# Four edits in a linear-attention and neighbourhood-attention kernel: column-ordered evacuation of the second group's queries, PSUM pairs in another order, shorter ring copies, and a later load of half the next image

## The chip, the cores and the metric

The program runs on one core of one Trainium2 chip. It is one launch that does the whole batch of sixteen images. The metric is device microseconds from start to end, the median of three runs. One more execution was taken with the hardware profiler; every duration below is from that one.

## The reference

Two residual layers act on x of shape (16, 64, 64, 256), and each starts with a group norm over 32 groups of channels.

```
x = x + linear_attention(gn(x))       # 8 heads of 32, softmax of q over d, of k over the 4096 pixels
x = x + neighbourhood(gn(x))          # 8 heads of 32, 7x7 window around each pixel
```

In the second layer, each pixel's query is multiplied with the 49 keys of its window, to which a learnt position embedding is added: for heads 0 to 3 it depends on the row of the window, for heads 4 to 7 on the column.

```
kp = unfold(k, 7) + e                        # e: emb0 by window row, emb1 by window column
attn = softmax(einsum(q, kp)) ;  out = einsum(unfold(v, 7), attn)
```

Everything is float32.

## The kernel before

The sixteen images are done one after the other in one loop. Channels lie on the partitions in two halves of 128, pixels in the free dimension, cut into eight strips of 512 (strip 0 is made of the image's two edges, 5 and 3 columns wide; the other strips are 8 columns by 64 rows). One image goes through these stages:

1. **Layer 0** (`layer0`): queries and keys by matmul (L514), `exp` on ACT (L518), the context matrix (L532), transposes (L546), and the output product (L587), which DVE adds to the image (L596) while it gathers statistics (L473).
2. **Positions and values** of layer 1: `positional_products` and `positional` put the products of queries and position embeddings into rows 0 to 63 of the tile `qq`; `store_rings` (L658) copies them to DRAM buffers `pos` so that `load_rings` (L665, L666) can read them back as a band with a different shift in each row; `values` (L677, L680) computes v and stores it to the DRAM buffer `vpad` (L685, L690), from which `load_window` (L731) fetches the windows `vw`.
3. **Keys and queries of head group 0** (`keys_queries(b, 0, x)`): eight groups of eight matmul passes (L703), four for keys and four for queries, each into two PSUM banks; ACT (L619) or DVE (L621) moves each result of 32 partitions by 512 to SBUF, adding the bias. Keys go to `kaug`, queries to `qq`.
4. **Attention of group 0** (`local_attention(b, 0, ...)`): four units of sixteen image columns, each with nine row blocks c. TensorE computes scores (L760) into a double PSUM tile, ACT takes `exp` (L768), TensorE sums weights and weighted values (L791) into the four single banks, which it first clears (L778, once a unit). At a unit's end `finish` divides and POOL adds to the output (L824).
5. **The same two stages for head group 1.** In its attention the statistics and the norm of the next image are worked in.

The order of instructions on each of PE, ACT, DVE and SP is the order in which the program issues them (`manual_schedule`), and each engine runs its own in order. All transfers are issued by SP, one queue in program order. Semaphores hold an instruction until the tiles that it needs are there or free.

[...] `double` is two tiles of two banks (pd), `single` four tiles of one (ps). `banks()` hands out four pairs in turn and says which engine evacuates each half (0 is DVE, 1 is ACT):

```
i = turn[1] % 4
if i % 2:
    return single[i - 1 : i + 1], (0, 1)
return [double[i // 2][:, j] for j in range(2)], (i // 2, i // 2)
```

So the turns are pd0 (both halves by DVE), ps0 and ps1 (one each), pd1 (both by ACT), ps2 and ps3 (one each). A double tile counts as one tile: its evacuation starts when the matmuls of both halves are done. `psum2()` hands out the double tiles alternately to the scores.

`qq` holds a group-0 query as (row, column) and a group-1 query as (column, row). A strip's result comes out of the matmul as 64 rows of 8 columns in both groups. `evacuate` therefore writes, for group 1, each element 64 elements (256 bytes) away from the one before it.

`between0` and `between1` are called by `local_attention` after each of the five steps g of each unit i; they issue loads, stores and statistics of the next image at that point of the order. Before the change the next image's second half is loaded by `load_half(b + 1, 1)` (L463, eight transfers of 256 KB) ahead of `keys_queries(b, 0, x)`.

Of the kernel before, what the change touches and what calls it, by code (L numbers as in the profile page):

```python
# [20 lines left out]
W = 64  # L21
C = 256
HEADS, HD = 8, 32
NS = 8
# [331 lines left out]
def attention_fast(tc, io, ok):  # L356
# [3 lines left out]
    with ExitStack() as ctx:  # L360
# [11 lines left out]
        def banks():  # L372

            i = turn[1] % 4
            turn[1] += 1
            if i % 2:
                return single[i - 1 : i + 1], (0, 1)
            return [double[i // 2][:, j] for j in range(2)], (i // 2, i // 2)

        def bank(name):  # L380
            return psum2()[:, 0]
# [114 lines left out]
        def by_rows(a, like):  # L496

            return a.rearrange("p (g r) w -> p g r w", g=4) if len(like.shape) == 4 else a
# [117 lines left out]
        def evacuate(i, dst, src, bias):  # L616

            if i:
                nc.scalar.activation(dst, src, AF.Identity, bias=bias)  # L619
            else:  # L620
                nc.vector.tensor_scalar(dst, src, bias, None, ALU.add)  # L621
# [27 lines left out]
        def store_rings():  # L649

            line = SLOTS * 4 * W
            for hg in range(2):
                for a in range(4):
                    for o in (0, RING):
                        row = pos[hg][RING * a, o]
                        dst = bass.AP(row.tensor, row.offset, [[W, 4 * KS], [line + 4 * W, RING], [1, W]])
                        src = qq[32 * hg : 32 * hg + 4 * KS, 0, 1024 * a : 1024 * (a + 1)]
                        nc.sync.dma_start(dst, src)  # L658

        def load_rings(hg):  # L660
# [33 lines left out]
        def keys_queries(b, hg, x):  # L694

            for what in range(2):
                for i in range(0, NS, 2):
                    ps, engines = banks()
                    pair = KEYED[i : i + 2]
                    wgt = wq if what else wk  # L700
                    for a in range(2):
                        for k in range(2):
                            nc.tensor.matmul(  # L703
                                ps[a],
                                wgt[:, k, hg * P : (hg + 1) * P],
                                x[k][:, strip(pair[a])],
                                start=(k == 0),
                                stop=(k == 1),
                            )
                    for a in range(2):  # L710
                        for h in range(4):
                            rows = slice(h * HD, (h + 1) * HD)
                            d0 = 64 * (h % 2)
                            for u, p0, m, w, view in pieces(pair[a]):
                                src = view(ps[a][rows])
                                if what:
                                    dst = placed(qq[d0 : d0 + HD, h // 2], hg)[:, :, w : w + m]
                                else:
                                    dst = kaug[h // 2][d0 : d0 + HD, u, PAD : PAD + W, p0 : p0 + m]
                                evacuate(engines[a], by_rows(dst, src), src, bias[rows, 2 * what + hg : 2 * what + hg + 1])  # L720

        def load_window(b, hg, t):

# [130 lines left out]
        with tc.manual_schedule(engines=ORDERED):  # L854
            x, xn = halves(0)
            st = stats_tile("st0_0")
            for k in range(2):
                load_half(0, k)
            for k in range(2):
                for s in ORDER:  # L860
                    strip_stats(st, x, k, s)
            gn = n.group_stats(st, 1e-5, small, bank, "0_0")
            xtok = {q: load_tokens(0, q) for q in range(2)}
            for s in ORDER[:2]:
                normalise(xn, x, *gn, s)
            for b in range(B):
                more = b + 1 < B
                x, xn = halves(b)
                st = layer0(b, x, xn, *gn, xtok, 2)
                mean, rstd = n.group_stats(st, 1e-5, small, bank, f"1_{b}")  # L870
                scale(wpos, n.wpos, rstd)
                pairs = [ORDER[i : i + 2] for i in range(0, NS, 2)]
                positional_products(0, x, pairs[0])
                pb = bank("fold")
                fold_bias(mean, wpos, (4,), pb)
                scale(wv, n.wv_sb, rstd)
                for i in range(4):
                    if i < 3:
                        positional_products(i + 1, x, pairs[i + 1])
                    positional(i, pairs[i])  # L880
                pv = bank("foldv")
                for k in range(2):
                    nc.tensor.matmul(
                        pv[:, :C], mean[:, k : k + 1].to_broadcast([P, P]), wv[:, k], start=(k == 0), stop=(k == 1)
                    )
                nc.vector.tensor_tensor(bv, n.bv_sb, pv[:, :C], ALU.subtract)
                store_rings()
                for i, s in enumerate(KEYED):
                    values(b, s, x)
                    if i == 1:  # L890
                        scale(wk, n.wk_sb, rstd)
                        scale(wq, n.wq_sb, rstd)
                    if i == 3:
                        load_rings(0)
                pb = bank("fold2")
                fold_bias(mean, wk, (0, 1), pb)
                fold_bias(mean, wq, (2, 3), pb)
                vw = {i: load_window(b, 0, UNITS[i]) for i in range(2)}
                if more:
                    load_half(b + 1, 1)  # L900
                    st = stats_tile(f"st0_{b + 1}")
                    x_next, xn_next = halves(b + 1)
                keys_queries(b, 0, x)
                y = [xn[0], x[1]]
                vw1 = {}

                def store_out(hg, i):

                    for s in ((3,), (4, 5), (6, 7), (1, 2, 0))[i]:
                        nc.sync.dma_start(out[b, :, hg, strip(s)], y[hg][:, strip(s)])  # L910

                def between0(i, g):
                    if g == 4:
                        if i >= 2:
                            vw1[i - 2] = load_window(b, 1, UNITS[i - 2])
                        store_out(0, i)
                    if more and i and g < 3 and 3 * (i - 1) + g < NS:
                        strip_stats(st, x_next, 1, ORDER[3 * (i - 1) + g])

                local_attention(b, 0, x, y, vw, lambda: load_rings(1), between0)  # L920
                keys_queries(b, 1, x)
                if more:
                    load_half(b + 1, 0)
                steps, gn, xtok = None, [], {}

                def between1(i, g):
                    nonlocal steps
                    if g == 4:
                        if more and i >= 2:
                            xtok[i - 2] = load_tokens(b + 1, i - 2)  # L930
                        store_out(1, i)
                    if not more:
                        return
                    if i == 1 and g < 4:
                        for s in ORDER[2 * g : 2 * g + 2]:
                            strip_stats(st, x_next, 0, s)
                    if i == 2 and g == 0:
                        steps = n.group_steps(st, 1e-5, small, next_bank, f"0_{b + 1}", gn)
                    if i == 2 and g < 3:
                        next(steps, None)  # L940
                    if i == 3 and g in (1, 2):
                        normalise(xn_next, x_next, *gn, ORDER[g - 1])

                local_attention(b, 1, x, y, vw1, lambda: None, between1)

            m = small.tile([P, 4], F32, tag="range", name="range")
            nc.gpsimd.memset(m, 0.0)
            for i, total in enumerate((tops, others)):
                nc.vector.tensor_reduce(m[:, i : i + 1], total, AX.X, ALU.add)
            nc.vector.tensor_reduce(m[:, 3:4], m[:, :3], AX.X, ALU.add)  # L950
            pm = bank("range_t")
            nc.tensor.transpose(pm[:1, :P], m[:, 3:4], n.ident)
            worst = small.tile([1, 1], F32, tag="worst", name="worst")
            nc.vector.tensor_reduce(worst, pm[:1, :P], AX.X, ALU.add)
            nc.vector.tensor_scalar(ok, worst, 1e30, None, ALU.is_le)
# [376 lines left out]
```

## Time and profile before

| what | value |
|---|---|
| median of three runs | 6140.36 us (6137.88 to 6141.98) |
| the profiled execution, its time and its span | 6124.67 us, 6122.9 us |
| PE busy | 5477.6 us (89% of the span) |
| PE weight loads busy | 3748.6 us (61%) |
| DVE, ACT, POOL busy | 2963.6 us (48%), 2358.4 us (39%), 1029.9 us (17%) |
| mean granted TensorE clock | 0.964 of full |
| moved by DMA | 536.12 MB, 88 GB/s mean |

Engines overlap, so the busy shares do not add up. One image takes about 378 us. A time such as "1517.20" is in us from the span's start. In a timeline row the first number is the start, the second the length, then engine, line, operation, tiles and shapes, and in brackets the idle time before the row with what ended it. In a row of waits the numbers are the total, how often, and the longest.

### The profile page before, as it was taken

The numbers are of one execution on the slowest core, as the hardware profiler recorded it, in microseconds if no ns is written. First come the engines' busy times: TensorE is split into PE (matmuls) and PEld (weight loads), VectorE is DVE, ScalarE is ACT, GpSimd is POOL, SyncE is SP. The second block draws the span as 40 slices with busy tenths as digits, with TensorE's granted clock in tenths as the row PEclk, the third lists the DMA queues.
The fourth block names the chain that finished last, engine by engine and source line by source line (L and its number), as shares of the span: only waits on it lengthen the run. The fifth ranks groups of instructions, "written<-read, shape, count | busy, mean of one in ns | idle before, by whom it ended". The sixth has DMA issues, their size and how long they took to land.

```text
span 6122.9 us, 171756 instructions
## 1 busy us (share of the span) xinstructions
PE 5477.6 (89%) x76913; PEld 3748.6 (61%) x76913; DVE 2963.6 (48%) x5034; ACT 2358.4 (39%) x3233; POOL 1029.9 (17%) x1945
## 2 busy tenths in 40 slices
PE   4989999898998989889898998988989999898997
PEld 2565665655656556665666656566565665656656
DVE  2544545545355454554544554454544545445354
ACT  0251443515335153351623425244252443515335
POOL 2012120211202112021120201212012120211202
PEclk9999999999999999999999999999999999999999
DMA  4341723416244252442515434163341723417234
GB/s 114 83 96 37 138 77 87 104 44 137 59 93 108 50 121 58 104 98 64 115 49 116 92 79 101 43 126 87 84 96 37 136 79 86 103 37 145 59 79 81
DMA packets 772876, 536.12 MB, mean 88 GB/s; under 512 B 276240, under 2 KB 703504, under 8 KB 769552
## 3 DMA queue, kind: packets, MB, share of 16 engines
q1 hardware_dynamic: 772128, 525.04, 38.8%
q8 instruction: 605, 9.91, 0.7%
q14 instruction: 143, 1.17, 0.1%
HBM read 357.02 MB, written 167.90 MB: 86 GB/s over the span
## 4 chain that ended last, share of the span: by engine, by line
PE 79%; ACT 6%; DMA 5%; SPq 4%; issue 4%; DVE 2%; POOL 0%; ACTq 0%; DVEq 0%; POOLq 0%
PE pd L760 15%; PE ps L791 15%; PE pd L514 14%; PE ps L532 7%; ACT qq L619 5%; PE pd L703 4%; PE pd L587 4%; PE ps L587 4%; PE ps L703 3%; PE pd L677 3%; PE ps L677 3%; PE ps L630 2%; DMA vpad<-v 2%; PE ps L546 2%; DMA vw<-vpad 2%
## 5 line engine op out<-in xcount | busy, mean ns | idle before, releaser
L768 ACT ACTIVATE e<-pd 128x896 f32<-128x896 f32 (+2 forms) x1152 | 926.5, 839 | 1078.3 <-PE pd L760 1077.3
L760 PE MATMUL pd<-qq,kaug 64*64 64x224 f32 (+5 forms) x27648 | 1044.8, 293 | 313.0 <-ACT qq L619 152.6
L760 PEld LDWEIGHTS pd<-qq,kaug 64*64 64x64 f32 x27648 | 918.9, 139 | 453.0 <-ACT qq L619 179.1
L514 PE MATMUL pd<-wqkv,img 128*128 128x512 f32 x2048 | 923.0, 595 | 1.6 <-DVE img L283 1.6
L791 PE MATMUL ps<-e,ones 128*32 128x112 f32 (+1 forms) x18432 | 835.6, 253 | 58.5 <-issue 57.9
L791 PE MATMUL ps<-e,vw 128*32 128x112 f32 (+1 forms) x18432 | 838.9, 256 | 54.0 <-issue 53.5
L804 DVE STREAM_TRANSPOSE r<-ps 128x512 f32<-128x512 f32 x256 | 168.7, 696 | 1415.1 <-PE ps L791 1415.1
L619 ACT ACTIVATE qq<-ps,bias 32x512 f32<-32x512 f32 (+2 forms) x544 | 370.1, 725 | 759.2 <-PE ps L630 711.6
L518 ACT ACTIVATE eq<-pd 128x1024 f32<-128x1024 f32 x256 | 261.9, 1023 | 943.5 <-PE pd L514 943.4
L451 POOL TENSOR_TENSOR others<-others,rc 128x16 f32<-128x16 f32 x256 | 113.0, 441 | 3045.1 <-DVE rc L809 3045.1
L514 PEld LDWEIGHTS pd<-wqkv,img 128*128 128x128 f32 x2048 | 372.6, 191 | 380.2 <-issue 352.8
L791 PEld LDWEIGHTS ps<-e,vw 128*32 128x32 f32 x18432 | 494.4, 111 | 139.9 <-issue 101.9
L791 PEld LDWEIGHTS ps<-e,ones 128*32 128x32 f32 x18432 | 536.8, 112 | 68.8 <-issue 67.9
L521 DVE TENSOR_REDUCE qz<-eq 128x16 f32<-128x512 f32 x256 | 175.5, 685 | 830.0 <-ACT eq L518 830.0
L532 PE MATMUL ps<-xtok,eq 128*128 128x257 f32 x2048 | 486.1, 380 | 0.0
L532 PEld LDWEIGHTS ps<-xtok,eq 128*128 128x128 f32 x2048 | 386.1, 190 | 149.0 <-issue 107.2
L824 POOL TENSOR_TENSOR img<-img,r 128x320 f32<-128x320 f32 (+1 forms) x512 | 421.5, 843 | 165.2 <-DVE rc L809 161.4
L619 ACT ACTIVATE kaug<-ps,bias 32x192 f32<-32x192 f32 (+2 forms) x384 | 196.8, 551 | 633.3 <-PE ps L703 630.0
L621 DVE TENSOR_SCALAR qq<-ps,bias 32x512 f32<-32x512 f32 x384 | 351.7, 916 | 8.7
L473 DVE BATCH_NORM_STATS2 st<-img 128x6 f32<-128x512 f32 x512 | 321.2, 677 | 66.4 <-DMA img<-in_xc 66.3
L524 POOL TENSOR_TENSOR eq<-eq,qr 128x512 f32<-128x512 f32 x256 | 274.7, 1073 | 30.7 <-DVE qr L523 1.2
L621 DVE TENSOR_SCALAR qq<-pd,bias 32x512 f32<-32x512 f32 x256 | 236.0, 922 | 29.7 <-PE pd L703 24.8
(126 smaller groups left out, 6269.8 us busy)
## 6 DMA issues: line engine op xcount, KB each, us to landing
vw<-vpad SPq DMA_DIRECT2D x512, 288.0 KB
img<-in_xc SPq DMA_DIRECT2D x256, 256.0 KB
xtok<-in_xt SPq DMA_DIRECT2D x64, 1024.0 KB
out<-img SPq DMA_DIRECT2D x256, 256.0 KB
vpad<-v SPq DMA_DIRECT2D x112, 512.0 KB
qq<-pos SPq DMA_DIRECT2D x128, 256.0 KB
qq<-in_ring SPq DMA_DIRECT2D x128, 256.0 KB
pos<-qq SPq DMA_DIRECT2D x256, 112.0 KB
```

Source lines behind the costliest of these rows:

```text
L473: nc.vector.bn_stats(st[:, k, s], x[k][:, strip(s)])
L514: nc.tensor.matmul(ps[:, t], xn[k][:, n0 : n0 + P], n.wqkv_sb[:, k, : 2 * C], start=(k == 0), stop=(k == 1))
L532: nc.tensor.matmul(pc[hg][:, : C + 1], eq[p][:, t, C + hg * P : C + (hg + 1) * P], xtok[p // 4][:, 2 * (p % 4) + t], start=(p == 0 and t = ...
L587: nc.tensor.matmul(py[co], w2[:, hg, co * P : (co + 1) * P], qq[:, hg, strip(s)], start=(hg == 0), stop=(hg == 1),)
L619: nc.scalar.activation(dst, src, AF.Identity, bias=bias)
L621: nc.vector.tensor_scalar(dst, src, bias, None, ALU.add)
L677: nc.tensor.matmul(pi[:, t], x[k][:, n0 : n0 + P], wv[:, k], start=(k == 0), stop=(k == 1))
L703: nc.tensor.matmul(ps[a], wgt[:, k, hg * P : (hg + 1) * P], x[k][:, strip(pair[a])], start=(k == 0), stop=(k == 1),)
L760: nc.tensor.matmul(to, kaug[pl][rows, u, 8 * c : 8 * c + 8].rearrange("p r w -> p (r w)"), q, start=True, stop=True,)
L768: nc.scalar.activation(e, ps[:, :, : 2 * m], AF.Exp)
L791: nc.tensor.matmul(dst, ones if to is zs[j] else vw[:, j, c, h * HD : (h + 1) * HD], pr, start=False, stop=(c == NB - 1),)
L824: nc.gpsimd.tensor_tensor(yv, xv, by_rows(add[:, :, a - w0 : e - w0], xv), ALU.add)
```

## The change

There are four edits.

- **Columns.** In `keys_queries`, for the queries of group 1 alone, both sides of the evacuation are reordered so that columns are the outer loop and rows the inner one. The destination in `qq` is then one contiguous run (512 elements, or 320 and 192 for the two pieces of strip 0), and the source in PSUM is read with a step of 8 elements (5 or 3 in strip 0).
- **Pairs.** `banks()` hands out pd0, pd1, ps0 with ps1, ps2 with ps3. It is used by L587, by `values` and by `keys_queries`. Which engine evacuates which tile stays the same.
- **Ring copies.** Each of the four pieces of a head group is still copied twice by `store_rings`, but the second copy holds its last 6 rows only, not 16 (42 KB, not 112 KB); the full copy now comes first.
- **Half image.** `load_half(b + 1, 1)` goes. Its eight strips are issued in `between0`, four in unit 0 and four in unit 1, after steps 0 to 3. The statistics of these strips, which stood in units 1 to 3 (three, three and two), now stand in units 2 and 3 (four each).

```
--- before.py
+++ after.py
@@ banks
             turn[1] += 1
-            if i % 2:
-                return single[i - 1 : i + 1], (0, 1)
-            return [double[i // 2][:, j] for j in range(2)], (i // 2, i // 2)
+            if i >= 2:
+                return single[2 * i - 4 : 2 * i - 2], (0, 1)
+            return [double[i][:, j] for j in range(2)], (i, i)
@@ store_rings
-                    for o in (0, RING):
-                        row = pos[hg][RING * a, o]
-                        dst = bass.AP(row.tensor, row.offset, [[W, 4 * KS], [line + 4 * W, RING], [1, W]])
-                        src = qq[32 * hg : 32 * hg + 4 * KS, 0, 1024 * a : 1024 * (a + 1)]
+                    for o, r in ((RING, 0), (0, RING - KS + 1)):
+                        row = pos[hg][RING * a + r, o + r]
+                        dst = bass.AP(row.tensor, row.offset, [[W, 4 * KS], [line + 4 * W, RING - r], [1, W]])
+                        src = qq[32 * hg : 32 * hg + 4 * KS, 0, W * (RING * a + r) : W * RING * (a + 1)]
                         nc.sync.dma_start(dst, src)
@@ keys_queries
-                                evacuate(engines[a], by_rows(dst, src), src, bias[rows, 2 * what + hg : 2 * what + hg + 1])
+                                dst = by_rows(dst, src)
+                                if what and hg:
+                                    order = "p r w -> p w r" if len(src.shape) == 3 else "p g r w -> p w g r"
+                                    dst, src = dst.rearrange(order), src.rearrange(order)
+                                evacuate(engines[a], dst, src, bias[rows, 2 * what + hg : 2 * what + hg + 1])
@@ attention_fast
                 if more:
-                    load_half(b + 1, 1)
                     st = stats_tile(f"st0_{b + 1}")
@@ between0
-                    if more and i and g < 3 and 3 * (i - 1) + g < NS:
-                        strip_stats(st, x_next, 1, ORDER[3 * (i - 1) + g])
+                    if more and g < 4:
+                        s = ORDER[4 * (i % 2) + g]
+                        if i < 2:
+                            nc.sync.dma_start(x_next[1][:, strip(s)], xc[b + 1, :, 1, strip(s)])
+                        else:
+                            strip_stats(st, x_next, 1, s)
```

## The prediction

> **What bounds the kernel now.** I read the busy shares first (PE 89%), then the waits of PE, then the timelines of one image around each wait, then instruction durations by shape. The PE waits that the change can touch:
>
> ```profile
> PE pd L760 <- ACT qq L619: 152.6, 32, 6.8
> PE ps L791 <- issue: 111.4, 73, 3.3
> PE pd L760 <- ACT e L768: 79.7, 32, 2.5
> PE pd L760 <- issue: 72.8, 49, 3.1
> ```
>
> The first and third come 32 times, twice an image: after each `keys_queries`, PE stands until ACT has emptied PSUM. The second and fourth are stalls inside the attention that no semaphore explains. PE at the two seams of image 3 (counted from 0), group 0 then group 1:
>
> ```profile
> 1414.74 3.60 PE L703 MATMUL ps<-img,wqn 128*128 128x512 f32 x8
> 1421.07 1.59 PE L760 MATMUL pd<-qq,kaug 64*64 64x80 f32 x48 [2.73 <-ACT qq L619]
> ...
> 1513.60 3.60 PE L703 MATMUL ps<-img,wqn 128*128 128x512 f32 x8
> 1523.99 2.79 PE L760 MATMUL pd<-qq,kaug 64*64 64x80 f32 x48 [6.79 <-ACT qq L619]
> 1529.27 3.27 PE L760 MATMUL pd<-qq,kaug 64*64 64x140 f32 x48 [2.50 <-ACT e L768]
> ```
>
> ACT at the second seam:
>
> ```profile
> 1510.37 4.55 ACT L619 ACTIVATE qq<-ps,bias 32x512 f32<-32x512 f32 x4 [1.28 <-PE ps L703]
> 1514.93 9.01 ACT L619 ACTIVATE qq<-pd,bias 32x512 f32<-32x512 f32 x8
> 1523.96 4.64 ACT L619 ACTIVATE qq<-ps,bias 32x320 f32<-32x320 f32 x8
> 1528.62 1.41 ACT L768 ACTIVATE e<-pd 128x512 f32<-128x512 f32 x2
> ```
>
> Call E the end of the last L703 (1517.20). ACT evacuates without a gap to E+11.4; PE's first scores wait for pd1 (E+6.8), the third for the first `exp` (E+12.1). ACT's sixteen query evacuations set the end here. DVE ends at E+7.5, so it doesn't. By shape in that stage:
>
> ```profile
> L619 ACT ACTIVATE qq<-pd,bias 32x512 f32<-32x512 f32 x8 | 8.9, 1115 | 0.1
> L619 ACT ACTIVATE kaug<-pd,bias 32x512 f32<-32x512 f32 x8 | 5.4, 678 | 0.8 <-PE pd L703 0.7
> ```
>
> Same size, same source: 678 ns into a contiguous row, 1115 ns with a 256-byte step in SBUF (741 ns in group 0, runs of 8).
>
> The chain of waits also shows "DMA vpad<-v", "DMA vw<-vpad" and "DMA img<-in_xc" (2% each for the first two). I take these as no limit: the link from "img<-in_xc" to an evacuation at 1423.22 falls where ACT had worked without a gap since 1415.00, PE runs unbroken from 1361 to 1418 but for 0.5 us, and no first L791 of a group waits for a DMA.
>
> [...] no run shows ACT or DVE reading PSUM with a step. [...] its clock records show the drop from about 2.0 us of idle in a window. [...] The page has 605 packets of 9.91 MB on q8[...].
>
> **Columns.** Writes become contiguous, reads get a 32-byte step in PSUM. Bounds for one 512 instruction: 678 ns (reading costs nothing more) to well over 1115[...]. I take 678[...]. ACT's query chain: 12 x 1.12 + 4.64 = 18.2 us becomes 12 x 0.69 (start to start) + 3.47 (what the eight pieces of strip 0 cost into `kaug`) = 11.7. ACT starts it at E-6.8 as now, since the matmuls set that. So `exp` starts at E+4.9, not E+11.4: **-6.45 us an image, -103 us**. DVE drops from 1.10 to about 0.75, ends near E+2.7, and is still not last.
>
> **Pairs.** In L587 and `values` all halves go to DVE, which waits for PE before every group; pd1 as second tile needs L886 (ends 1363.23), and its group starts at 1364.5. Cost nothing; if that cover went, some 1 us an image. In `keys_queries` ACT's first tile is now pd1, ready when ps1 was (both end the second pair). Group 0's queries then run 6.01 + 3.01 + 3.43 without the 0.44 us gap before pd1: `exp` starts at E+5.7, not 6.14: -0.45 us. pd1 is free at E-0.8, so the first two scores run at E, not E+2.73. What is late next is `exp`, behind ACT's evacuations: PE's two idle pieces of 2.73 and 2.48 us become one from E+1.6 to E+6.3, 4.7 us. That costs clock:
>
> ```profile
> 1424.70:1432.00 7.30, 6.86 (x232) 6.09 (x236) 0.00 (x0) 4.65 (x6) 0.00 (x0) 1.00 0.01 3
> 2176.30:2183.60 7.30, 6.87 (x174) 5.96 (x178) 0.00 (x0) 3.80 (x5) 0.00 (x0) 0.77 0.02 4
> ```
>
> The same stretch after the seam in images 3 and 5: full clock (1.00) and 232 matmuls, half clock in part (0.77) and 174. In 6 of 16 images group 0 has one half-clock window there; from E to the second unit's clearing (L778) it takes 24.32 us, the ten others 22.76. So 3.41 us at half clock cost 1.56 us, 46%. A 4.7 us gap always puts 2.0 us into one window, and holds the clock down some 4.2 us past the gap (the grid's average, estimated): 1.93 us, for 6/16 x 1.56 = 0.59 now. Group 0: -0.45 + 1.93 - 0.59 = **+0.9 us an image, +14 us**. Group 1 is at half clock after all 16 seams already (1.63 us); with the gap E+1.6 to E+5.5 about 1.9: **+4 us** in all.
>
> **Ring copies.** Eight transfers an image lose 28 x 10 packets of 256 bytes: 2240, at the 700 packets per us seen from 1364 to 1373, 3.2 us of queue. The rings are issued by 1390.9 and used at 1421, the windows' data end at 1417.5 and are used at 1427: the slack hides it. Zero; bounds 0 to -3.2 us an image.
>
> **Half image.** The four loads of unit 0 have no wait but their queue's own lanes; SP issues them right after the windows, when it does now (1411 on). The four of unit 1 stand behind the store of unit 0, which waits for POOL (issued 1446.00), so they go at 1446.4 to 1448, behind a window's burst. There the cost is code fetch:
>
> ```profile
> 1445.82 0.36 PE L791 MATMUL ps<-e,ones 128*32 128x112 f32 x4
> 1448.50 0.39 PE L791 MATMUL ps<-e,ones 128*32 128x112 f32 x4 [2.32 <-issue]
> ```
>
> A 16 KB fetch starts about every 3.6 us; during the window burst from 1440 to 1447.5 the next after 1439.5 starts only at 1445.82, and PE stalls. Units without a burst have no such stall in any image; those with one have 2.06 us (one output strip of 256 KB behind it), 2.25 (two strips). Four strips more by that slope: 0.6 to 0.8 us; a stall that fills a clock window adds 1.56 at times. I take +0.9. Bounds: 0 (the next fetch, near 1450, comes when the data have passed) to 4.2 (2.6 us, half of the 5.2 that eight strips took from 1417.4, plus 1.56). Behind these loads in SP's queue is the window of unit 3, not issued before 1456.77, so nobody waits. The last image has none: 15 x 0.9 = **+14 us**. The statistics change places in DVE time that is idle; that is free, and without that cover it would be 0.6 us each.
>
> **Sum.** -103 + 4 + 14 + 14 = -71 us against the profiled 6124.67 us: 6053. The median is 0.26% above that execution, so 6140.36 - 71 = **6069 us**.
>
> **Rivals.**
> - *The PSUM step is as dear as the SBUF step.* [...] The columns bring 0, the rest stays: +28, **6168 us**, slower than before. It decides from about 1000 ns per evacuation: 437 ns less saves 6.45 us, so 28/16 = 1.75 us an image is 0.12 us below 1.12.
> - *It is dearer still*, say 1.5 us: 16 evacuations' worth, another 6 us an image: **6265 us**.
> - *The loads hurt more.* At the bound of 4.2 us an image: +63, not +14: **6118 us**.
> - *The DMA part of the chain is real*, and shorter ring copies move the start: 3.2 x 16 = 51 us more: **6018 us**. Against it speak the gapless PE and the missing wait for a window.
>
> **How the numbers follow.** Forecast 58% (its own range 6035 to 6100, from the clock's luck and the load bound); PSUM as dear 22%; dearer 7%; loads 8%; DMA real 5%. Range 6035 to 6185: it takes in the forecast but for its tail, the first and the third rival; it leaves out the second, the fourth and some tails. Within 0.2% (12 us, about what a measurement here can tell from no change) is 5%, the tails of rivals one and three; faster 69%, slower 26%.
>
> **What would show it.** The columns: `qq` evacuations of group 1 at about 680 ns on ACT and 750 on DVE, `exp` at E+4.9; 1.1 us or more there makes the forecast wrong. The pairs: no wait of L760 on L619 at either seam (a long one in group 1 under the first rival), one wait on `exp` of about 4.7 us in group 0, half clock after all 32 seams. The loads: a longer stall in unit 1 of group 0 than 2.06 us, the other units as they are. The rings: half of the copies at 42 KB, and L587 to L703 as long as now.

## The result and the profile after

The changed kernel takes 6059.36 us (median of four runs, 6045.62 to 6069.72) against 6141.17 us before (four runs): 0.9869 of the time, 95% interval 0.9846 to 0.9891, so 67 to 95 us less. Its profiled execution took 6068.61 us with a span of 6066.8 us; it is among the longer of its runs, and the profiled execution of the kernel before (6124.67 us) was shorter than any of the four that were timed. The two profiles are therefore only 56 us apart. Sizes below are taken from the timed ratios, places from the profiles.

The waits of PE (engine, line, what it waited for, us in total, times, longest), in the changed kernel. Lines have moved: L760 is L766, L791 is L797, L768 is L774, L703 is L704 and L778 is L784.

```profile
PE pd L766 <- ACT e L774: 143.5, 32, 4.9
PE ps L797 <- issue: 122.3, 76, 3.4
...
PE pd L766 <- issue: 67.0, 52, 3.3
```

The wait of the scores for ACT's evacuations (152.6 us before) is gone, and the wait for `exp` has grown from 79.7 to 143.5. Together the two fell by 88.8 us, more than the 56 us between the profiles. The rest was lost again: PE is busy for 5506.4 us, not 5477.6, with the same number of matmuls (76913), and its stalls without a releaser ("issue") grew by 5.1 us. PE's timeline at the two seams of image 3, group 0 then group 1:

```profile
1402.09 1.49 PE L766 MATMUL pd<-qq,kaug 64*64 64x80 f32 x48
1408.49 3.27 PE L766 MATMUL pd<-qq,kaug 64*64 64x140 f32 x48 [4.91 <-ACT e L774]
...
1503.79 1.50 PE L766 MATMUL pd<-qq,kaug 64*64 64x80 f32 x48
1509.34 3.14 PE L766 MATMUL pd<-qq,kaug 64*64 64x140 f32 x48 [4.06 <-ACT e L774]
```

The first two scores now follow the last L704 without a wait. One idle gap is left at each seam, and the scores after it take 3.27 and 3.14 us for 48 passes, where the same 48 take 1.80 at full clock (in a run below). ACT at the seam of group 1, whose last L704 ends at 1503.86:

```profile
1497.03 5.52 ACT L619 ACTIVATE qq<-pd,bias 32x512 f32<-32x512 f32 x8 [1.95 <-PE pd L704]
1502.57 6.10 ACT L619 ACTIVATE qq<-ps,bias 32x512 f32<-32x512 f32 x12
1508.69 1.41 ACT L774 ACTIVATE e<-pd 128x512 f32<-128x512 f32 x2
```

Eight evacuations take 5.52 us instead of 9.01, and `exp` starts 4.8 us after E, not 11.4. By shape, ACT in the same stage, and DVE over the whole run, where its evacuations from pd into `qq` took 922 ns on average before:

```profile
L619 ACT ACTIVATE qq<-pd,bias 32x512 f32<-32x512 f32 x8 | 5.4, 678 | 2.0 <-PE pd L704 1.9
...
L619 ACT ACTIVATE qq<-ps,bias 32x320 f32<-32x320 f32 x4 | 2.1, 519 | 0.1
...
L621 DVE TENSOR_SCALAR qq<-pd,bias 32x512 f32<-32x512 f32 x256 | 191.2, 747 | 30.8 <-PE pd L704 25.4
```

678 ns is, to the nanosecond, what the evacuation into `kaug` takes, which reads PSUM in one contiguous run. DVE's 747 ns is likewise what it takes into `kaug`. Reading with a step of 32 bytes has no price here, on either engine. Why a step costs ACT 437 ns in SBUF and nothing in PSUM, no run shows. For the step of 20 bytes in strip 0 no run has the same write without the step. By the 0.85 ns an element that `exp` shows (597 ns for 512, 914 to 924 for 896) 320 elements would take about 515 ns, an estimate, and 519 were measured.

### The profile page after: what moved, and what is told of

Its sections match the earlier page's. It is cut to its first block, busy times and chain, and to the rows that moved or that the text cites. A ratio compares the mean times of both kernels' runs of the same rounds, so it can differ in the third digit from the quotient of the medians.

```text
span 6066.8 us, 171741 instructions
## 1 busy us (share of the span) xinstructions
PE 5506.4 (91%) x76913; PEld 3771.3 (62%) x76913; DVE 2874.6 (47%) x5034; ACT 2254.7 (37%) x3233; POOL 1029.9 (17%) x1945
## 3 DMA queue, kind: packets, MB, share of 16 engines
q8 instruction: 605, 9.91, 0.7%
HBM read 357.02 MB, written 158.73 MB: 85 GB/s over the span
## 4 chain that ended last, share of the span: by engine, by line
PE 88%; ACT 4%; issue 4%; DVE 2%; SPq 1%; DMA 0%; POOL 0%; ACTq 0%; DVEq 0%; POOLq 0%
PE pd L766 16%; PE ps L797 16%; PE pd L514 15%; PE pd L704 7%; PE ps L532 7%; PE ps L704 5%; ACT qq L619 4%; PE pd L587 4%; PE ps L678 4%; PE pd L678 4%; PE ps L587 4%; PE ps L630 2%; PE ps L546 2%; PE ps L784 1%; SPq L399 1%
## 5 line engine op out<-in xcount | busy, mean ns | idle before, releaser
L774 ACT ACTIVATE e<-pd 128x896 f32<-128x896 f32 (+2 forms) x1152 | 928.5, 839 | 1132.0 <-PE pd L766 1129.4
L766 PE MATMUL pd<-qq,kaug 64*64 64x140 f32 (+5 forms) x27648 | 1052.3, 294 | 218.4 <-ACT e L774 143.5
L766 PEld LDWEIGHTS pd<-qq,kaug 64*64 64x64 f32 x27648 | 923.8, 140 | 354.4 <-issue 163.6
L797 PE MATMUL ps<-e,vw 128*32 128x112 f32 (+1 forms) x18432 | 853.8, 260 | 63.4 <-issue 63.0
L797 PE MATMUL ps<-e,ones 128*32 128x112 f32 (+1 forms) x18432 | 846.5, 256 | 59.7 <-issue 59.2
L797 PEld LDWEIGHTS ps<-e,vw 128*32 128x32 f32 x18432 | 502.9, 113 | 154.9 <-issue 117.7
L797 PEld LDWEIGHTS ps<-e,ones 128*32 128x32 f32 x18432 | 546.5, 114 | 72.4 <-issue 71.8
L619 ACT ACTIVATE qq<-ps,bias 32x512 f32<-32x512 f32 (+2 forms) x544 | 320.2, 622 | 718.1 <-PE ps L630 712.5
L619 ACT ACTIVATE kaug<-pd,bias 32x512 f32<-32x512 f32 x256 | 173.7, 679 | 633.6 <-PE pd L704 630.7
L621 DVE TENSOR_SCALAR qq<-ps,bias 32x512 f32<-32x512 f32 x384 | 309.3, 806 | 6.8
L821 DVE TENSOR_TENSOR r<-r 128x512 f32<-128x512 f32 x256 | 222.3, 868 | 27.5 <-DVE r L817 0.5
```

What stands on the lines that cost most here:

```text
L766: nc.tensor.matmul(to, kaug[pl][rows, u, 8 * c : 8 * c + 8].rearrange("p r w -> p (r w)"), q, start=True, stop=True,)
L774: nc.scalar.activation(e, ps[:, :, : 2 * m], AF.Exp)
L797: nc.tensor.matmul(dst, ones if to is zs[j] else vw[:, j, c, h * HD : (h + 1) * HD], pr, start=False, stop=(c == NB - 1),)
```

## The experiments

All experiments but `cols_both` were timed 5 to 14 times beside the kernel before (9 or 23 times); of `cols_both` there is one execution, the profiled one. The table is worked out from the timelines of all sixteen images of each profile, as means. E is the end of the last matmul of `keys_queries`; "exp" is the start of the first `exp` after it; "to 2nd unit" is the time from E to the clearing (L778) of the second unit; "half clock" says after how many of sixteen seams the clock records show half clock (a granted share of 0.5) past the start of `exp`; "stall" is the time in which PE stands without a releaser in unit 1 of group 0 (units are counted from 0, so unit 1 is the second).

| kernel | ratio to before | group 0: exp, to 2nd unit, half clock | group 1: exp, to 2nd unit, half clock | stall |
|---|---|---|---|---|
| before | 1 | 6.16, 23.34, 6 | 11.44, 29.86, 16 | 2.06 |
| changed | 0.9869 | 5.69, 24.73, 16 | 4.83, 23.57, 16 | 2.43 |
| cols_only | 0.9826 | 6.17, 23.75, 10 | 5.51, 23.35, 12 | 2.00 |
| pairs_only | 1.0030 | 5.70, 24.68, 16 | 11.49, 30.34, 16 | 1.76 |
| half_only | 1.0027 | 6.16, 23.61, 7 | 11.45, 30.02, 16 | 2.64 |
| rings_only | 1.0006 | 6.17, 23.91, 11 | 11.47, 30.52, 16 | 2.09 |
| no_pairs | 0.9831 | 6.17, 23.50, 7 | 5.51, 23.06, 9 | 2.53 |
| warm_after | 0.9757 | 5.69, 22.40, 0 | 4.83, 21.50, 0 | 2.68 |
| best1 | 0.9712 | 5.27, 22.03, 0 | 4.26, 20.91, 0 | 1.94 |
| best2 | 0.9663 | 5.28, 22.05, 0 | 4.27, 20.94, 0 | 2.45 |
| cols_both | one execution | 11.39, 30.02, 16 | 5.50, 23.16, 10 | 1.88 |

### One part at a time

**The columns alone.** The edit in `keys_queries`, nothing else:

```
-                                evacuate(engines[a], by_rows(dst, src), src, bias[rows, 2 * what + hg : 2 * what + hg + 1])
+                                dst = by_rows(dst, src)
+                                if what and hg:
+                                    order = "p r w -> p w r" if len(src.shape) == 3 else "p g r w -> p w g r"
+                                    dst, src = dst.rearrange(order), src.rearrange(order)
+                                evacuate(engines[a], dst, src, bias[rows, 2 * what + hg : 2 * what + hg + 1])
```

> The kernel before with the column order alone. Theory (contiguous writes pay, the stepped PSUM read costs nothing): group-1 evacuations of 512 at about 680 ns on ACT instead of 1115, the first exp of group 1 at E+5.3 us (with the 0.44 us gap that the old pair order leaves) instead of E+11.4, about -6.1 us an image from that. The first two scores of group 1 then run from about E+2.1, when pd1 is empty, so the idle time is in two pieces as in group 0 before, and the half clock comes after only some of the sixteen seams: about another -1 us an image. Sum -100 to -115 us. Rival (the gain of the whole change came from pairs or rings): less than -60 us.

Measured: 6036.01 us against 6147.36, ratio 0.9826 (0.9802 to 0.9849): 93 to 122 us less. The waits of PE in this kernel:

```profile
PE pd L765 <- ACT qq L619: 78.7, 32, 2.7
PE pd L765 <- ACT e L773: 72.0, 32, 2.5
```

Group 1 now looks like group 0 before: two gaps of at most 2.7 and 2.5 us, `exp` at E+5.51, and half clock after 12 of 16 seams, not all. The columns carry the whole gain and more; the rival, under 60 us, falls. Group 0, which this edit does not touch, shows half clock after 10 seams where the kernel before shows 6. The other kernels with the same seam of group 0 show 7 (half_only), 11 (rings_only) and 7 (no_pairs), so the number varies by chance, and 6 is the lowest of the five.

**The pairs alone.**

```
-            if i % 2:
-                return single[i - 1 : i + 1], (0, 1)
-            return [double[i // 2][:, j] for j in range(2)], (i // 2, i // 2)
+            if i >= 2:
+                return single[2 * i - 4 : 2 * i - 2], (0, 1)
+            return [double[i][:, j] for j in range(2)], (i, i)
```

> The kernel before with the pair order alone. Theory (half clock after the joined gap): group 0 waits once for exp, about 4.7 us, at half clock afterwards in all sixteen images; in the profile of the whole change this made E to the second clearing 24.7 us instead of 23.35 on average. Group 1 stays as before, since its exp waits for the same ACT chain. Sum +14 to +25 us. Rival (the gap of 0.44 us that closes is all there is): -7 us.

Measured: 6165.98 us against 6147.36, ratio 1.0030 (1.0017 to 1.0043): 10 to 26 us slower. `exp` of group 0 comes 0.46 us earlier, as worked out, and yet the second unit starts 1.34 us later on average; half clock follows all sixteen seams, where it followed six. Against the mean of the four other kernels with the old seam (23.69 us) the loss is 0.99 us. That the clock is the cause is tested below.

**The later loads alone.**

```
-                    load_half(b + 1, 1)
...
+                        s = ORDER[4 * (i % 2) + g]
+                        if i < 2:
+                            nc.sync.dma_start(x_next[1][:, strip(s)], xc[b + 1, :, 1, strip(s)])
...
```

> The kernel before with the later load of half the next image alone. Theory (the loads lengthen the code-fetch stall of unit 1 in group 0): stall there about 2.5 us instead of 2.06, and now and then a half-clock window more, +6 to +14 us in all. Rival (hidden): within 5 us of the kernel before. Rival (they hurt badly): +30 us or more.

Measured: 6160.5 us against 6147.36, ratio 1.0027 (1.0014 to 1.0040): 9 to 25 us slower. The unexplained stall in unit 1 grew from 2.06 to 2.64 us and the unit from 17.37 to 18.20; in the four profiles that have the later loads the unit takes 18.16 to 18.22 us, in the other seven 17.06 to 18.03. 0.58 of the 0.83 us is the stall. The size of the stall alone would not decide, since best2, which lacks the later loads, has 2.45 us. The number of stalls decides more: in the four profiles with the later loads PE stalls for over 0.8 us without a releaser 20 to 22 times in unit 1 of group 0, in the other seven 15 or 16 times, over the sixteen images. In that unit 2.44 MB move on average in half_only, 1.45 in the kernel before. The waits of PE in half_only (73 and 111.4 us before):

```profile
PE ps L791 <- issue: 124.6, 93, 3.6
```

The traces also show what such a stall follows. In the kernel before, each of the 88 stalls of over 0.8 us inside the attention ends 1.23 to 1.82 us after a packet on queue q8 has landed; in half_only the 93 end 1.24 to 1.90 us after one. The page lists q8 as "instruction", with 605 packets and 9.91 MB (each has 16 KB); these are the code fetches of the prediction. Of PE's instructions in the attention, taken at regular intervals, only 17% start 1.1 to 1.9 us after a landing. That PE waits there for its code is inferred from these times. That the data transfers delay the fetch is argued from times as well: unit 0 of group 0, which has no burst beside it, has no such stall in either profile. No experiment of its own shows it.

**The shorter ring copies alone.**

```
-                    for o in (0, RING):
+                    for o, r in ((RING, 0), (0, RING - KS + 1)):
...
```

> The kernel before with the shorter ring copies alone. Theory (these transfers have slack): within 5 us of the kernel before; the same waits of PE. Rival (the DMA part of the chain of waits is real): up to -51 us.

Measured: 6154.68 us against 6147.36, ratio 1.0006 (0.9992 to 1.0019): no difference that can be told. 9 MB less are written (167.90 to 158.73 MB by the page's count), and PE waits as long as before (150.2 us for the evacuations, 80.0 for `exp`; 152.6 and 79.7 before). So these copies were not a limit.

The four parts alone add up to -1.74 + 0.30 + 0.27 + 0.06 = -1.11%, and the whole is -1.31% (-1.54 to -1.09): they don't interact beyond what can be measured here, where each of the four has an interval of its own of 0.13% to 0.24% to either side.

### Taking the pairs out again, and taking the idle gap's clock away

**The changed kernel with the old pair order.**

```
-            if i >= 2:
-                return single[2 * i - 4 : 2 * i - 2], (0, 1)
-            return [double[i][:, j] for j in range(2)], (i, i)
+            if i % 2:
+                return single[i - 1 : i + 1], (0, 1)
+            return [double[i // 2][:, j] for j in range(2)], (i // 2, i // 2)
```

> The changed kernel with the old pair order (columns, shorter rings and the later loads stay). Theory (the pair order costs clock): E to the second clearing back near 23.5 us in group 0 (24.73 in the changed kernel) and 23.35 in group 1, so about 20 us faster than the changed kernel: 0.984 of the kernel before. Rival (pairs help once the columns are there, by the earlier exp of 0.68 us in group 1): 0.988 or more.

Measured: 6037.96 us, ratio 0.9831 (0.9806 to 0.9857). With `exp` 0.48 us later in group 0 and 0.68 us later in group 1, the second units start 1.23 and 0.51 us earlier. By the two ratios it is some 23 us faster than the changed kernel, just clear of their intervals (2 to 44). The rival asked for 0.988 or more and falls.

**Filling the gap.** If half clock is what the pairs cost, work of no use in the idle time should give it back:

```
                     if step == len(groups) - 1:
                         after_scores()
+                    if step == 0:
+                        for _ in range(14):
+                            nc.tensor.matmul(single[0], zb, zb[:, :1].to_broadcast([P, 512]), start=True, stop=True)
```

> The changed kernel with 14 matmuls more at each seam, which clear the bank ps0 after the first two scores, in the time in which PE waits for exp; the first real clearing of the unit overwrites what they write. Theory (the cost of the pair order is half clock after a joined idle gap): no half clock at the seams, z0 + first unit 22.3 us in group 0 (24.73) and 21.4 in group 1 (23.57), about -70 us against the changed kernel, 0.977 of the kernel before. Rival (the later scores or exp themselves are slower, clock plays no part): no gain, or a loss where these matmuls end after exp.

Measured: 5990.23 us against 6136.53, ratio 0.9757 (0.9731 to 0.9784), some 69 us faster than the changed kernel by the two ratios (47 to 90, worked out from their intervals). PE at the seam of group 0 in image 3 of this kernel:

```profile
1402.68 1.49 PE L766 MATMUL pd<-qq,kaug 64*64 64x80 f32 x48
1404.11 3.22 PE L843 MATMUL ps<-zb 128*128 128x512 bf16 x14
1409.09 1.80 PE L766 MATMUL pd<-qq,kaug 64*64 64x140 f32 x48 [1.76 <-ACT e L774]
```

The 48 passes after the gap take 1.80 us, not 3.27. Windows of the two kernels over the 7.4 us after `exp` of both groups (length; busy us and count of PE, weight loads, DVE, ACT and POOL; then the granted clock, the DMA share and GB/s), the changed kernel:

```profile
1407.80:1415.20 7.40, 6.71 (x152) 5.90 (x156) 0.00 (x0) 3.26 (x5) 0.00 (x0) 0.63 0.01 2
1508.70:1516.10 7.40, 6.76 (x179) 6.16 (x183) 0.00 (x0) 4.12 (x6) 0.00 (x0) 0.77 0.02 4
```

and the one with the gap filled:

```profile
1408.40:1415.80 7.40, 6.71 (x228) 5.99 (x228) 0.00 (x0) 4.88 (x7) 0.00 (x0) 1.00 0.01 3
1505.10:1512.50 7.40, 6.69 (x228) 5.99 (x228) 0.00 (x0) 4.90 (x7) 0.00 (x0) 1.00 0.02 6
```

PE is busy for as long in all four, and does 152 and 179 matmuls at clocks of 0.63 and 0.77, 228 at full clock. `exp` starts where it did (5.69 and 4.83), so ACT's part did not change. This shows the clock to be the cost of the joined gap: with the clock kept full, group 0's second unit starts at 22.40 us, before the 23.50 of the old pair order. Filling the two gaps of the old pair order was not tried.

### Both steps in one instruction

One execution: the column order for group 0 too, where it makes the write the stepped one.

```
-                                if what and hg:
+                                if what:
```

> The kernel before with the column order for the queries of both groups: in group 0 this writes SBUF with a step of 256 bytes and reads PSUM with a step of 32 bytes in one instruction. If the PSUM step is free, such an instruction takes what the SBUF step alone took, about 1115 ns on ACT and 1090 on DVE (741 and 750 in group 0 before); if it has a price that the contiguous write hides, more than 1200 ns. The seam of group 0 then has exp near E+11.4 and costs about 6 us an image: about as slow as the kernel before.

Measured: the profiled execution took 6123.02 us. ACT around the seam of group 0:

```profile
L619 ACT ACTIVATE qq<-pd,bias 32x512 f32<-32x512 f32 x8 | 8.9, 1112 | 0.1
L619 ACT ACTIVATE qq<-ps,bias 32x512 f32<-32x512 f32 x4 | 4.5, 1130 | 1.4 <-issue 1.3
```

A step of 256 bytes in SBUF and one of 32 bytes in PSUM cost together what the first costs alone: 1112 ns, against 1115 for the write with the step in group 1 before. The seam of group 0 took over the shape of the old seam of group 1 (`exp` at E+11.39), so the layout decides which of the groups pays.

### Versions that beat both kernels

The columns, the pairs with the gap filled, the shorter rings (which neither gain nor lose), no later loads, and strip 0 given to DVE. Of the edits the one that is new here:

```
-                    pair = KEYED[i : i + 2]
+                    pair = (KEYED[:6] + (0, 1))[i : i + 2]
```

> Columns, pairs, shorter rings and the 14 matmuls of the run above; the half image loaded as in the kernel before; and in keys and queries strip 0, whose eight pieces cost ACT 3.47 us for 2.75, changes place with strip 1, so that DVE evacuates it. Theory (ACT's chain sets the seam, the loads cost 1 us an image): exp at E+5.0 in group 0 and E+4.1 in group 1, no half clock at the seams, 0.972 of the kernel before. Rival (DVE becomes last at the seam): no gain over the run with the matmuls beyond the loads.

Measured: 5960.08 us against 6136.53, ratio 0.9712 (0.9686 to 0.9738). `exp` comes at E+5.27 and E+4.26, 0.2 us later than worked out and 0.4 to 0.6 earlier than in the run before. DVE does not become last: in group 1 of image 3 it ends at 1496.98 and ACT at 1498.08. What leaving out the later loads and moving strip 0 are worth each was not measured apart in this kernel.

The same filling was then put into the wait for the statistics after layer 0:

```
                 st = layer0(b, x, xn, *gn, xtok, 2)
+                for _ in range(11):
+                    nc.tensor.matmul(single[0], zb, zb[:, :1].to_broadcast([P, 512]), start=True, stop=True)
```

> best1 with 11 such matmuls more in each image, right after the last output product of layer 0, where PE waits 2.7 us for the statistics. Theory (that wait turns the clock to half for two of its windows, and the work that follows starts at a window's end, which is why the seam of group 0 lies at nearly the same place of the clock's grid in all sixteen images, a spread of 1.0 us of 3.41): no half clock after the norm, some 2.1 us an image less (4.6 us of position products at half clock x 0.46), 0.966 to 0.967 of the kernel before; and the ends of the last L703 of group 0 spread over the whole grid. Rival (the place on the grid has another reason): the spread stays near 1.0 us.

Measured: 5940.01 us against 6139.93, ratio 0.9663 (0.9646 to 0.9681), the fastest of all. But the reason that was given for it is not borne out: half clock still follows the norm in 13 of 16 images. It sets in later, after the position products (L630) have begun, whose passes take 681 ns on average instead of 718 in best1. From the end of the last output product to the end of the position products an image is 0.7 us shorter in the profiles, some 12 of the 30 us that the ratios differ by, so where the rest comes from is open. The ends of group 0's L703 spread over 1.5 us of the clock's grid, not 1.0 and not 3.41. Why they lie so close together stays open too.

## Why the prediction held

**Columns: right, in mechanism and size.** The open question was the price of the stepped read. The value taken, 678 ns, was the author's estimate, since no run before showed such a read; it is also what was measured. DVE's evacuations went to 747 ns, as put. The forecast for this part was -103; alone it measured -107 (-93 to -122). The +4 for the clock at group 1's seam belongs to the joined gap and so to columns and pairs together: from `exp` to the second unit the changed kernel takes 18.74 us there (23.57 less 4.83), the kernel before 18.42, some 5 us over sixteen images. The first and second rival, PSUM as dear as SBUF or dearer, are out. (In the working, 12 x 1.12 + 4.64 is 18.1; 18.2 is what the timeline gives, from 1510.37 to 1528.62.)

**Pairs: right in sign and cause, with two terms too small that partly cancel.** +14 was put down for group 0; alone they measured +18 (+10 to +26). The first term that was off is the half clock past the gap: "some 4.2 us, the grid's average" stood for 1.93 us. In the profile after, half clock starts 4.3 to 5.2 us after E in all sixteen images and lasts 6.83 us, so it ends 4.8 to 5.7 us past the gap; the second unit's start at 24.73 us is 2.44 us over the 22.29 of a full clock (22.76 less the 0.47 by which `exp` is earlier). The grid's average was the wrong measure, since the seam of group 0 lies within 1.0 us of a 3.41 us grid in every image. The trace of the kernel before shows this already: there E lies 0.9 to 1.8 us before the end of one of the clock's windows in all sixteen images. The second term is what is lost already, 0.59 us an image from 6 half-clock windows in sixteen. The five profiles with the old seam have 8.2 on average, which makes 0.80. With -0.47 for the earlier `exp`, 2.44 and 0.80 the sum is +1.17 us an image, or +19 us, against the +18 measured. So the second error hid part of the first, which is luck.

The half clock from about 2.0 us of idle in a window, by which the prediction goes, comes out of the trace of the kernel before. All changes of its granted clock, between 1 and 0.5, lie on one grid of 3.413 us, to 0.01 us, over 6 ms. From 0.1 ms after the start on, a window at full clock in which PE's matmuls left 2.0 us or more idle was followed by half clock in 56 of 57 cases, one with 1.25 to 2.0 us in 13 of 100, one with less than 1.25 us in none of 1477. After half clock, a window with 0.74 us or more idle was followed by half clock again in 56 of 56.

**Later loads: right.** +14 was put, +17 (+9 to +25) measured. The places are as foretold: four transfers issued at 1393.23, right behind the windows, and four behind the store of unit 0. The stall of unit 1 became longer, as foretold. SP's queue in the changed kernel:

```profile
1385.80 7.39 SPq L737 DMA_DIRECT2D vw<-vpad  x8
1393.23 2.80 SPq L925 DMA_DIRECT2D img<-in_xc  x4
1424.96 3.27 SPq L737 DMA_DIRECT2D vw<-vpad  x4
1431.49 0.35 SPq L915 DMA_DIRECT2D out<-img  x1
1431.89 2.48 SPq L925 DMA_DIRECT2D img<-in_xc  x4
```

The rival that they hurt more (+63 us) is out.

**Ring copies: right.** Zero was put, +4 (-5 to +12) measured. The chain of waits had 5% of DMA before, has 3% with the shorter copies alone and 0% both with the later loads alone and in the changed kernel. So it was the later loads that took DMA out of the chain, and they made the kernel slower: that share was no limit. The fourth rival (51 us more) is out.

**The sum.** -71 us was forecast and -81 (-67 to -95) measured, and for each of the four parts what was put lies within the interval that was measured for it alone; the predicted 6069 us lies 10 us above the median, within what a measurement here can tell.

## What to carry to other kernels

When an evacuation has to turn a layout, try the step on the PSUM side and write SBUF in one run: here a step in PSUM was free and one in SBUF cost 64% (678 to 1115 ns). When an edit joins two short idle gaps of TensorE into one, count the clock with it: 0.47 us won on ACT was lost about four times over at half clock (2.44 us less the 0.59 of before), and matmuls of no use in the gap were worth some 69 us. An edit made of several parts should be taken apart, since here two of the four cost 35 us of what the first brought.

## What the runs showed of the hardware

ACT and DVE read PSUM with a step of 32 bytes in 678 and 747 ns for 32 by 512, the same as a contiguous read. Fourteen bf16 matmuls of zeros, 3.2 us in a gap of 4.9, kept the granted clock at 1.00 after all 32 seams, so they count as work for the clock. In the kernel before, a clock window of 3.413 us with 2.0 us or more of idle time was followed by half clock in 56 of 57 cases, and one window at half clock cost 1.56 us of the attention's work (24.32 us from E to the second unit, not 22.76). Inside the attention of that kernel PE stood 88 times for over 0.8 us without a releaser, and each of these stalls ends 1.23 to 1.82 us after a packet of the instruction queue q8 has landed; in unit 1 of group 0, which has a burst of data transfers beside it, PE stood for 2.06 us an image. That the place of group 0's seam on the clock's grid is nearly the same in all images (E lies 0.9 to 1.8 us before the end of a window) was not expected and is not explained.
